# An attention and Hadamard-FFN kernel on one core: the first three output tiles formed group by group

## The chip, the cores and the metric

The kernel runs on one core of a Trainium2 chip. The metric is the device time of one execution in microseconds, as the median of several executions. A core has TensorE (PE: matmuls, and PEld: its weight loads), VectorE (DVE), ScalarE (ACT), GpSimd (POOL) and SyncE (SP), which in this kernel issues every DMA. Each engine works through its own instructions in order and waits on semaphores where it needs another's result.

## The reference

4096 rows of 512 go through linear attention with 16 heads of 128 in 4 key/value groups, an output projection `Wo`, an addition and a layer norm, then a gated FFN whose inputs are Hadamard transformed, an addition and a layer norm:

```python
qf = jax.nn.elu(q) + 1.0;  kf = jax.nn.elu(k) + 1.0      # after rotary embedding
def step(carry, inp):
    state, z = carry
    q_s, k_s, v_s = inp
    state = state + k_s[..., :, None] * v_s[..., None, :]
    z = z + k_s
    num = jnp.einsum('bhe,bhed->bhd', q_s, state)
    den = jnp.einsum('bhe,bhe->bh', q_s, z)[..., None] + EPS
    return ((state, z), num / den)
...
attn = out.transpose(1, 0, 2, 3).reshape(bsz, seq_len, H * HD) @ Wo.T
x = _layernorm(x + attn)
...
x = fwht(x * SU_ug) / SCALE
x = silu(x @ W_gate.T * s_gate) * (x @ W_up.T * s_up)
x = fwht(x * SU_dp) / SCALE
x = _layernorm(x_in + x @ W_down.T * s_down)
```

## The kernel before

All values are fp32. A matmul operand is split into a high half and a low remainder (`hilo`, L93: ACT copies the rounded high half, L94; DVE or POOL subtracts it from the value, L95), and each product is three matmuls: high by high, high by low, low by high.

**Attention** (L183 to L735) walks the sequence in blocks. Its 128 slots, `i` = 0 to 127, are a hand-written order: at each slot the source names what starts there, and instructions marked with `pin` or with a third argument `True` of `dma` keep their place in the order of the source. All other instructions are put in order by the compiler's scheduler, engine by engine. The attention leaves numerators (`num_d`, 32 tiles of 128 rows by 4 groups by 512) and denominators (`den_d`) in DRAM; denominators come back later, are inverted and stored as factors (`rec_d`).

**Output tiles** (L854 to about L1005). For each of 32 tiles of 128 rows and each of 4 groups of heads: numerators are loaded (`nt`), the factors are loaded and broadcast to 128 partitions (`rb`, `pre_rb`, L144), `norm_o` (L860) multiplies the two, on DVE for even groups into a PSUM tile `ps_on` and on POOL for odd ones into `o32`, and splits the product. `wo_tile` (L173) then runs 48 matmuls of 128 by 512 into one PSUM bank: 4 groups by 4 heads by 3. The tile is added to the rows of `x` in `yp`; every second tile a layer norm follows and a generator (`wo_front`) of Hadamard work for the FFN is started, which is stepped from tile to tile. Loads run ahead: `pre(t + 2)` opens tile `t + 2`'s numerators, one DMA of 1 MB, and `pre_rb` is eight groups ahead. A further generator, `constants` (L877), loads the sign and scale vectors and the Hadamard matrix (`sut`, `had32`, `wsc`, `sudp`, `wsdp`) and prepares them; it is stepped once per tile from tile 0 on.

**The seam between the two.** The output weights come as 16 raw tiles of 128 by 512, one for each head (`wo_raw`, L111), and are split by `wo_split` (L115). Both start before attention ends: raw loads at slots 118 to 123, splits of heads 0 to 10 at slots 121 to 126, of heads 11 to 15 behind the last slot (L722 to L726). Raw tiles borrow memory that attention has done with: `praw` buffers, the freed x halves (`xh`, `xl`), a `vd` tile for heads 10 to 13, and two quarters of `ntx` for heads 14 and 15. Tile 0's four groups are multiplied and split by `o_load`, `o_mul` and `o_split` (L505 to L527) between slots 107 and 126, and tile 0 is formed alone behind the last slot, in a PSUM bank of the attention's pool (`ps_w0`). Tile 1's numerators are read in four pieces of 256 KB (`nt_part`), tile 0's too; every other tile's as one DMA. The attention's PSUM pools close with attention, and the output tiles' pools (`pfd`, `pon`, `pwo`) are opened after that.

All DMAs stand on SP's queue in one order. A DMA that waits, for its source to be computed or for the last reader of the memory that it will write, holds back every DMA behind it. Pools opened with `reuse_waits="tile"` lay their tiles over memory of closed pools; the first write to such a tile waits for the last reader of whatever lay there.

Of the kernel before, what the change touches and what calls it, by code (L numbers as in the profile page):

```python
# [43 lines left out]
def kernel(  # L44
# [96 lines left out]

    RB = {}

    def pre_rb(k):  # L144
        if k < 128:
            pool, m = (late["p"], 3) if k < 6 or (k - 8) % 5 < 3 else (late["c2"], 2)
            RB[k] = pool.tile([128, 512], F32, tag="rb", name="rb", bufs=m)
            dma(RB[k], rec_d[k // 4][k % 4 * 512:k % 4 * 512 + 512].partition_broadcast(128), k < 10)

# [7 lines left out]
    def pre(t):  # L157
        if 5 <= t <= 13 and t % 2:
            if t > 5:
                recip(*cur["dn"])  # L160
            if t < 13:
                cur["dn"] = recip_load(NB - 4 + (t - 5) // 2)
        cur[t] = dict(nt=late["p"].tile([128, 16, 128], F32, tag="nt", name="nt", bufs=2))
        if t == 1:
            nt_part(0)
        else:
            dma(cur[t]["nt"], num_d[t].rearrange("p g n -> p (g n)"), t < 3)
        pre_yp(t)

    def nt_part(g):  # L170
        dma(cur[1]["nt"][:, 4 * g:4 * g + 4], num_d[1][:, g], True)

    def wo_tile(t, ps, after=None, gs=range(KVH)):  # L173
        i = 12 * gs[0]
        for g in gs:
            oh, ol = cur[t][g]
            for h in range(4):
                wh, wl = WO[4 * g + h]
                for l, r in ((oh, wh), (oh, wl), (ol, wh)):
                    T.matmul(ps, l[:, h], r, start=i == 0, stop=i == 47)  # L180
                    i += 1
            if after is not None:
                after(g)  # L183


    with ExitStack() as es:
# [4 lines left out]
        p3 = es.enter_context(tc.tile_pool(name="a3", bufs=3))  # L191
        pmm = es.enter_context(tc.tile_pool(name="pmm", bufs=3, space=PSUM))
        psc = es.enter_context(tc.tile_pool(name="psc", bufs=1, space=PSUM))
        pnum = es.enter_context(tc.tile_pool(name="pnum", bufs=2, space=PSUM))
        pden = es.enter_context(tc.tile_pool(name="pden", bufs=1, space=PSUM))
        pst = es.enter_context(tc.tile_pool(name="pst", bufs=1, space=PSUM))

# [307 lines left out]

        def o_load(g, hi, lo):
            if g < 2:
                nt = praw.tile([128, 512], F32, tag="raw", name="nt0")
                dma(nt, num_d[0][:, g], True)
                rb = praw.tile([128, 512], F32, tag="raw", name="rb0")  # L510
                dma(rb, rec_d[0][g * 512:(g + 1) * 512].partition_broadcast(128), True)
            else:
                nt = ntx[:, g]
                dma(nt, num_d[0][:, g], True)
                pre_rb(g)
                rb = RB.pop(g)
            O0[g] = (hi, lo, nt, rb)

        def o_mul(g, eng=G):
            pin(eng.tensor_tensor(O0[g][3], O0[g][2], O0[g][3], ALU.mult))  # L520

        def o_split(g, eng):
            hi, lo, nt, rb = O0[g]
            if hi is None:
                hi, lo = (wres.tile([128, 4, 128], F32R, tag="w", name=x) for x in ("oh0", "ol0"))
            hilo(hi, lo, rb.rearrange("p (h n) -> p h n", h=4), eng, True)
            cur.setdefault(g // 4, {})[g % 4] = (hi, lo)  # L527

# [62 lines left out]
        for i, (n, g, p) in enumerate(slots):  # L591
# [78 lines left out]
            elif i == 118:  # L670
                for h in range(3):
                    wo_raw(h, praw.tile([128, 512], F32, tag="raw", name="woraw"))
            elif i == 119:
                for x in ("xh", "xl"):
                    x = pe.tile([128, 4, 256], F32, tag=x, name="woraw").rearrange("p a b -> p (a b)")
                    wo_raw(len(WR), x[:, 0:512])
                    wo_raw(len(WR), x[:, 512:1024])
            elif i == 121:
                wo_split(G, 0, 1)
                wo_split(V, 2)  # L680
                for h in range(7, 10):
                    wo_raw(h, praw.tile([128, 512], F32, tag="raw", name="woraw"))
            elif i == 122:
                wo_split(G, 3, 4)
                wo_split(V, 5)
                o2 = [p3.tile([128, 2, 4, 128], F32R, tag=t, name=t, bufs=4) for t in ("qh", "ql")]
            elif i == 123:
                wo_split(G, 6)
                early.close()
# [3 lines left out]
                for y in range(2):  # L693
                    o_load(2 + y, o2[0][:, y], o2[1][:, y])
                x = p2.tile([128, 4, 512], F32, tag="vd", name="woraw")
                for h in range(10, 14):
                    wo_raw(h, x[:, h - 10])
                for h in range(14, 16):
                    wo_raw(h, ntx[:, h - 14])
                pre_rb(4)  # L700
                pre_yp(0)
                pre(1)
            elif i == 124:
                wo_split(G, 7)
                wo_split(V, 8)
            elif i == 125:
                o_mul(2, V)
                wo_split(G, 9)
                o_mul(3, V)
            elif i == 126:  # L710
                o_split(2, V)
                o_split(3, V)
                pre_rb(5)
                wo_split(G, 10)
            if sl == (1, 1):
# [5 lines left out]

        for g in range(1, KVH):  # L722
            nt_part(g)
        wo_split(V, 11)
        wo_split(G, 12)
        wo_split(V, 13)  # L726
        wo_split(G, 15)
        wo_split(V, 14)
        O0[4] = (*(p3.tile([128, 4, 128], F32R, tag=x, name=x) for x in ("sh", "sl")),
                 cur[1]["nt"][:, 0:4].rearrange("p h n -> p (h n)"), RB.pop(4))  # L730
        o_mul(4)
        o_split(4, V)
        ps0 = pmm.tile([128, DM], F32, tag="mm", name="ps_w0")
        wo_tile(0, ps0)
        pin(V.tensor_tensor(cur[0]["yp"][:, 0], ps0, cur[0]["yp"][:, 0], ALU.add))  # L735

# [116 lines left out]

    with ExitStack() as es:  # L854
        p2 = late["c2"] = es.enter_context(tc.tile_pool(name="c2", bufs=2, reuse_waits="tile"))
        pfd = es.enter_context(tc.tile_pool(name="pfd", bufs=1, space=PSUM, reuse_waits="tile"))
        pon = es.enter_context(tc.tile_pool(name="pon", bufs=2, space=PSUM, reuse_waits="tile"))
        pwo = es.enter_context(tc.tile_pool(name="pwo", bufs=3, space=PSUM, reuse_waits="tile"))

        def norm_o(t, g):  # L860
            c = cur[t]
            rb = RB.pop(4 * t + g).rearrange("p (h n) -> p h n", h=4)
            if g % 2 == 0:
                o32 = pon.tile([128, 4, 128], F32, tag="on", name="ps_on")
                i = V.tensor_tensor(o32, c["nt"][:, 4 * g:4 * g + 4], rb, ALU.mult)
            else:
                o32 = p2.tile([128, 4, 128], F32, tag="o32", name="o32")
                i = G.tensor_tensor(o32, c["nt"][:, 4 * g:4 * g + 4], rb, ALU.mult)  # L868
            hi, lo = (p2.tile([128, 4, 128], F32R, tag="o", name=n, bufs=8) for n in ("oh", "ol"))
            if t == 1:  # L870
                pin(i)
            hilo(hi, lo, o32, V, t == 1)
            c[g] = (hi, lo)

# [79 lines left out]
        raws = []  # L954
        for t in range(32):
            if t + 2 < 32:
                pre(t + 2)
            def after(g):
                if t == 31:
                    for s in (2 * g, 2 * g + 1):  # L960
                        if s < 7:
                            asplit(0, s)
                if t + 1 < 32:
                    if t + g:
                        norm_o(t + 1, g)
# [12 lines left out]
            if t < 3:  # L978
                next(gc, None)
            cur.pop(t)  # L980
            if t % 2:
# [409 lines left out]
```

## Time and profile before

| What | us |
|---|---|
| median of 3 runs | 2179.8 (2177.97, 2179.8, 2180.97) |
| the profiled execution | 2179.87 |
| its span in the profile | 2178.2 |
| mean granted TensorE clock in it | 0.997 of full |
| DRAM read, written | 282.76 MB, 156.76 MB |

The page divides the span into 40 slices; a slice is 54.5 us long. Its digits are tenths of busy time, so a 9 means 90% or more. Where the prediction shows a window, the columns are its bounds in microseconds from the span's start, its length, the busy time and number of instructions of each engine, the granted clock, the share of DMA time and the rate moved. In a timeline row the columns are the start, the busy time, the engine, the source line, the operation, what is written and read, and in brackets the idle time before it and who ended that. Attention ends at about 853 us; tile 1's matmuls begin at 864.37. These are, from the timelines of DVE, POOL and SP, products that use loaded factors, and the DMAs that carry factors and numerators (for a DMA, the time is that of its issue on SP's queue):

```profile
848.61 0.69 DVE L520 TENSOR_TENSOR rb<-ntx,rb 128x512 f32<-128x512 f32 x1 [1.13 <-DMA rb<-rec_d]
...
867.77 0.70 DVE L865 TENSOR_TENSOR ps_on<-nt,rb 128x512 f32<-128x512 f32 x1
...
873.77 0.70 DVE L865 TENSOR_TENSOR ps_on<-nt,rb 128x512 f32<-128x512 f32 x1 [0.92 <-DMA rb<-rec_d]
```

```profile
870.17 1.29 POOL L868 TENSOR_TENSOR o<-nt,rb 128x512 f32<-128x512 f32 x1 [5.27 <-DMA rb<-rec_d]
```

```profile
843.43 0.43 SPq L58 DMA_DIRECT2D rb<-rec_d  x1
...
864.22 0.80 SPq L58 DMA_DIRECT2D rb<-rec_d  x2
865.12 0.36 SPq L58 DMA_DIRECT2D nt<-num_d  x1
865.53 0.43 SPq L58 DMA_DIRECT2D yp<-in_x_n_dram  x1
866.00 1.67 SPq L58 DMA_DIRECT2D rb<-rec_d  x3
```

The factors issued at 843.43 are used at 848.61 on DVE, which waited for them (5.2 us); of the two issued at 864.22, the first is used at 867.77 by DVE, which was not waiting for anything else (at most 3.5 us), the second, issued at about 864.6, at 870.17 by POOL, which waited (5.6 us); the first of the three at 866.00, behind a 1 MB piece of numerators, at 873.77 by DVE, which waited (7.7 us).

### The profile page before, as it was taken

The page shows a single profiled execution, that of the slowest core. Times are in us where ns is not written, and L with a number is a line of the kernel's source. Part 1 is how long each engine was busy: PE and PEld are TensorE (multiplying, and loading weights), DVE is VectorE, ACT ScalarE, POOL GpSimd, SP SyncE. Part 2 cuts the span into 40 slices and gives each one's busy share as a digit, 9 for nine tenths or more (in the row PEclk, how much of TensorE's full clock was granted, in tenths as well). Part 3 has the DMA queues.
Part 4 walks back from the last instruction along what each step waited for, and adds up shares of the span by engine and source line. Part 5 has one row for each costly group of instructions (what it writes and reads, how often), then busy time and mean ns, then how long its engine had stood idle before and what let it go on. Part 6 is the DMA issues. An engine that isn't in the chain of part 4 may idle for free.

```text
span 2178.2 us, 42193 instructions
## 1 busy us (share of the span) xinstructions
PE 2140.6 (98%) x14319; PEld 1947.6 (89%) x14319; DVE 1728.9 (79%) x2675; ACT 1378.9 (63%) x2490; POOL 1321.8 (61%) x1104
## 2 busy tenths in 40 slices
PE   8999999999999998999999999999999999999998
PEld 8999999999999997887788788888888888999998
DVE  8999999899999997888998766776866766675655
ACT  8877877777777775443444476655655655565554
POOL 5777767666666666487888256565655555543332
PEclk9999999999999999999999999999999999999999
DMA  6666666656666666989988886876766767897784
GB/s 225 214 221 212 225 220 200 211 183 196 190 201 202 208 187 226 348 245 292 281 289 265 272 277 219 248 243 196 248 207 193 249 191 211 263 307 256 234 261 140
DMA packets 360553, 503.88 MB, mean 231 GB/s; under 512 B 68012, under 2 KB 187052, under 8 KB 356498
## 3 DMA queue, kind: packets, MB, share of 16 engines
q1 hardware_dynamic: 360338, 501.19, 72.1%
q8 instruction: 113, 1.85, 0.4%
q14 instruction: 102, 0.84, 0.1%
HBM read 282.76 MB, written 156.76 MB: 202 GB/s over the span
## 4 chain that ended last, share of the span: by engine, by line
PE 68%; DVE 12%; DMA 7%; issue 4%; POOL 4%; ACT 3%; SPq 2%; DVEq 0%; POOLq 0%; ACTq 0%
PE ps_a L1117 14%; PE ps_qk L339 12%; PE ps_da L1298 8%; PE ps_b L1117 7%; PE ps_wo L180 7%; PE ps_num L468 4%; PE ps_db L1298 4%; PE ps_c L1117 4%; PE ps_v L287 2%; DMA rb<-rec_d 2%; PE ps_dc L1298 2%; SPq L58 2%; DVE ps_qk L322 1%; PE ps_s L391 1%; DMA yraw<-yq_d 1%
## 5 line engine op out<-in xcount | busy, mean ns | idle before, releaser
L339 PE MATMUL ps_qk<-xh,wh 128*128 128x256 f32 x1280 | 354.9, 277 | 1.6 <-DVE x L325 0.9
L339 PE MATMUL ps_qk<-xh,wl 128*128 128x256 f32 x1280 | 354.0, 277 | 0.0
L339 PE MATMUL ps_qk<-xl,wh 128*128 128x256 f32 x1280 | 353.7, 276 | 0.0
L1099 POOL TENSOR_TENSOR cc<-cc 128x512 f32<-128x512 f32 x96 | 146.1, 1525 | 270.4 <-ACT cc L1096 129.5
L95 DVE TENSOR_TENSOR wol<-A,woh 128x512 fp32r<-128x512 f32 x217 | 226.4, 1050 | 94.7 <-ACT woh L94 84.0
L448 POOL TENSOR_SCALAR_AFFINE_SELECT A<-A 64x512 fp32r<-64x512 f32 x256 | 202.7, 792 | 131.1 <-DVE am L444 91.2
L321 POOL TENSOR_TENSOR sw<-sw,csb 128x512 f32<-128x512 f32 x160 | 213.9, 1337 | 76.2 <-ACT sw L320 64.8
L339 PEld LDWEIGHTS ps_qk<-xh,wh 128*128 128x128 f32 x1280 | 240.5, 188 | 4.7 <-DVE ql L422 1.5
L339 PEld LDWEIGHTS ps_qk<-xh,wl 128*128 128x128 f32 x1280 | 240.5, 188 | 1.5 <-DVE wl L95 0.2
L339 PEld LDWEIGHTS ps_qk<-xl,wh 128*128 128x128 f32 x1280 | 240.4, 188 | 1.0
L94 ACT ACTIVATE woh<-A 128x512 fp32r<-128x512 f32 x217 | 135.0, 628 | 122.5 <-PE ps_b L1117 72.8
L1117 PE MATMUL ps_a<-yoh,woh 128*128 128x512 f32 x512 | 199.9, 391 | 3.1 <-ACT sv L1124 2.6
L95 POOL TENSOR_TENSOR hal<-hraw,hah 128x512 fp32r<-128x512 f32 x74 | 98.1, 1327 | 172.7 <-PE ps_da L1298 59.6
L1117 PE MATMUL ps_a<-yol,woh 128*128 128x512 f32 x512 | 199.4, 389 | 0.0
L94 ACT ACTIVATE hah<-hraw 128x512 fp32r<-128x512 f32 x212 | 132.1, 631 | 106.3 <-PE ps_da L1298 54.2
L1117 PE MATMUL ps_a<-yoh,wol 128*128 128x512 f32 x512 | 196.7, 390 | 0.0
L95 DVE TENSOR_TENSOR hal<-hraw,hah 128x512 fp32r<-128x512 f32 x138 | 99.2, 727 | 90.1 <-PE ps_da L1298 39.0
L1124 ACT ACTIVATE sv<-ps_a,wsc 128x512 f32<-128x512 f32 x192 | 126.8, 679 | 34.7 <-PE ps_a L1117 34.4
L180 PE MATMUL ps_wo<-wh,oh 128*128 128x512 f32 x368 | 144.4, 393 | 0.0
L180 PE MATMUL ps_wo<-wh,ol 128*128 128x512 f32 x368 | 144.0, 391 | 0.0
L180 PE MATMUL ps_wo<-wl,oh 128*128 128x512 f32 x368 | 143.5, 390 | 0.0
L868 POOL TENSOR_TENSOR o<-nt,rb 128x512 f32<-128x512 f32 x62 | 86.8, 1400 | 74.0 <-DVE ol L95 44.1
(306 smaller groups left out, 7274.4 us busy)
## 6 DMA issues: line engine op xcount, KB each, us to landing
hraw<-hop_d SPq DMA_DIRECT2D x224, 256.0 KB
num_d<-num SPq DMA_DIRECT2D x128, 256.0 KB
rb<-rec_d SPq DMA_DIRECT2D x128, 256.0 KB
hop_d<-hS SPq DMA_DIRECT2D x128, 256.0 KB
vd<-vhl SPq DMA_DIRECT2D x128, 252.0 KB
nt<-num_d SPq DMA_DIRECT2D x30, 1024.0 KB
A<-in_wug_dram SPq DMA_DIRECT2D x93, 256.0 KB
hop_d<-cc SPq DMA_DIRECT2D x64, 256.0 KB
```

Of the source, the lines that this page charges most:

```text
L94: i = S.activation(hi, src, AF.Copy)
L95: j = eng.tensor_tensor(lo, src, hi.bitcast(F32), ALU.subtract)
L180: T.matmul(ps, l[:, h], r, start=i == 0, stop=i == 47)
L321: G.tensor_tensor(sw, sw, sinb, ALU.mult)
L339: T.matmul(ps[:, j], W[key][wa][:, k * 128:(k + 1) * 128], B[xa][:, k], start=i == 0, stop=i == 11)
L448: G.affine_select(ah, ah.bitcast(F32), pattern=[[0, 8], [1, 64]], compare_op=ALU.is_ge, fill=0.0, base=0, channel_multiplier=-1)
L468: T.matmul(ps[:, c2], l, r, start=i == 0, stop=i == len(ops) - 1)
L868: i = G.tensor_tensor(o32, c["nt"][:, 4 * g:4 * g + 4], rb, ALU.mult)
L1099: G.tensor_tensor(x, x, c.pop(("g", q)), ALU.mult)
L1117: T.matmul(ps, w[:, u, k], y[:, k], start=first and i == 0, stop=i == 5, skip_group_check=not first)
L1124: S.activation(x, ps, AF.Copy, scale=sc)
L1298: T.matmul(pj[j], ops[qd][al][:, r, js], BW[s][bl][ip], start=first and (i == 0 or i == 3 and pj is ps), stop=i >= 45 or last and i == 23, ...
```

## The change

The matmuls and what they compute stay the same. What is changed is the order of the first 12 of 128 pairs of tile and group, and with it where the output weights are split.

- `SQ` lists the pairs: for `k` = 0 to 11 tiles 0, 1, 2 of group 0, then tiles 0, 1, 2 of group 1, and so on; from `k` = 12 on tile by tile as before. `RB`, `NT` and `OH` (factors, numerators, split products) are kept by `k` and by pair.
- Tiles 0, 1 and 2 are summed in three PSUM banks at the same time (`PS`). For that the attention's PSUM pools close and the output tiles' pools open ahead of the first output matmul.
- `wo_part(0)` to `wo_part(4)` stand behind the last slot of attention, the others in a loop over `k`; `done` adds `x` at `k` = 9, 10 and 11, and goes on with what the loop over the tiles did.
- Output weights: heads 0 to 5 are split at slots 123 to 126, heads 6 and 7 behind the last slot, heads 8 to 15 between `wo_part` 0 and 5. Raw tiles 3 to 6 lie in `wres` buffers, 10 to 13 in the `vd` tile as before, 9, 14 and 15 in `praw`.
- Numerators of tiles 0, 1 and 2 are read in twelve pieces of 256 KB; from tile 3 on, as one DMA of 1 MB each.
- `constants` is stepped at `k` = 0, 4 and 8, behind `pre` of tiles 2, 3 and 4.

```diff
-    RB = {}
+    RB, NT, OH = {}, {}, {}
+    SQ = [(t, g) for g in range(KVH) for t in range(3)] + [(t, g) for t in range(3, 32) for g in range(KVH)]
+
+    def rb_src(k):
+        t, g = SQ[k]
+        return rec_d[t][g * 512:(g + 1) * 512].partition_broadcast(128)
+
+    def nt_src(k):
+        t, g = SQ[k]
+        return num_d[t][:, g]
 
     def pre_rb(k):
         if k < 128:
             pool, m = (late["p"], 3) if k < 6 or (k - 8) % 5 < 3 else (late["c2"], 2)
             RB[k] = pool.tile([128, 512], F32, tag="rb", name="rb", bufs=m)
-            dma(RB[k], rec_d[k // 4][k % 4 * 512:k % 4 * 512 + 512].partition_broadcast(128), k < 10)
+            dma(RB[k], rb_src(k), k < 10)
...
-        cur[t] = dict(nt=late["p"].tile([128, 16, 128], F32, tag="nt", name="nt", bufs=2))
+        nt = late["p"].tile([128, 4, 512], F32, tag="nt", name="nt", bufs=2)
+        for g in range(4):
+            NT[4 * t + g] = nt[:, g]
         if t == 1:
-            nt_part(0)
+            nt_part(4)
+        elif t == 2:
+            for k in range(8, 12):
+                nt_part(k)
         else:
-            dma(cur[t]["nt"], num_d[t].rearrange("p g n -> p (g n)"), t < 3)
+            dma(nt, num_d[t])
         pre_yp(t)
 
-    def nt_part(g):
-        dma(cur[1]["nt"][:, 4 * g:4 * g + 4], num_d[1][:, g], True)
+    def nt_part(k):
+        dma(NT[k], nt_src(k), True)
 
     def wo_tile(t, ps, after=None, gs=range(KVH)):
         i = 12 * gs[0]
         for g in gs:
-            oh, ol = cur[t][g]
+            oh, ol = OH.pop((t, g))
             for h in range(4):
                 wh, wl = WO[4 * g + h]
                 for l, r in ((oh, wh), (oh, wl), (ol, wh)):
                     T.matmul(ps, l[:, h], r, start=i == 0, stop=i == 47)
                     i += 1
             if after is not None:
-                after(g)
-
+                after(4 * t + g)
...
+        es_ps = ExitStack()
+        pmm = es_ps.enter_context(tc.tile_pool(name="pmm", bufs=3, space=PSUM))
+        psc = es_ps.enter_context(tc.tile_pool(name="psc", bufs=1, space=PSUM))
+        pnum = es_ps.enter_context(tc.tile_pool(name="pnum", bufs=2, space=PSUM))
+        pden = es_ps.enter_context(tc.tile_pool(name="pden", bufs=1, space=PSUM))
+        pst = es_ps.enter_context(tc.tile_pool(name="pst", bufs=1, space=PSUM))
...
+        def o_split(k, eng):
+            hi, lo, nt, rb = O0.pop(k)
             if hi is None:
                 hi, lo = (wres.tile([128, 4, 128], F32R, tag="w", name=x) for x in ("oh0", "ol0"))
             hilo(hi, lo, rb.rearrange("p (h n) -> p h n", h=4), eng, True)
-            cur.setdefault(g // 4, {})[g % 4] = (hi, lo)
+            OH[SQ[k]] = (hi, lo)
...
-            elif i == 119:
-                for x in ("xh", "xl"):
-                    x = pe.tile([128, 4, 256], F32, tag=x, name="woraw").rearrange("p a b -> p (a b)")
-                    wo_raw(len(WR), x[:, 0:512])
-                    wo_raw(len(WR), x[:, 512:1024])
             elif i == 121:
-                wo_split(G, 0, 1)
-                wo_split(V, 2)
-                for h in range(7, 10):
-                    wo_raw(h, praw.tile([128, 512], F32, tag="raw", name="woraw"))
+                for h in range(3, 7):
+                    wo_raw(h, wres.tile([128, 512], F32, tag="w", name="woraw"))
             elif i == 122:
-                wo_split(G, 3, 4)
-                wo_split(V, 5)
                 o2 = [p3.tile([128, 2, 4, 128], F32R, tag=t, name=t, bufs=4) for t in ("qh", "ql")]
             elif i == 123:
-                wo_split(G, 6)
+                wo_split(G, 0, 1)
                 early.close()
                 late["s"] = ExitStack()
                 late["p"] = late["s"].enter_context(tc.tile_pool(name="cl", bufs=2, side="right", reuse_waits="tile"))
                 ntx = late["p"].tile([128, 4, 512], F32, tag="nt", name="ntx", bufs=2)
                 for y in range(2):
                     o_load(2 + y, o2[0][:, y], o2[1][:, y])
+                for h in range(7, 9):
+                    wo_raw(h, praw.tile([128, 512], F32, tag="raw", name="woraw"))
+                pre_rb(4)
+                pre_yp(0)
+                pre(1)
                 x = p2.tile([128, 4, 512], F32, tag="vd", name="woraw")
                 for h in range(10, 14):
                     wo_raw(h, x[:, h - 10])
-                for h in range(14, 16):
-                    wo_raw(h, ntx[:, h - 14])
-                pre_rb(4)
-                pre_yp(0)
-                pre(1)
             elif i == 124:
-                wo_split(G, 7)
-                wo_split(V, 8)
+                wo_split(V, 2)
+                wo_split(G, 3)
+                wo_raw(9, praw.tile([128, 512], F32, tag="raw", name="woraw"))
             elif i == 125:
                 o_mul(2, V)
-                wo_split(G, 9)
+                wo_split(G, 4)
                 o_mul(3, V)
             elif i == 126:
                 o_split(2, V)
                 o_split(3, V)
                 pre_rb(5)
-                wo_split(G, 10)
+                wo_split(G, 5)
...
-        for g in range(1, KVH):
-            nt_part(g)
-        wo_split(V, 11)
-        wo_split(G, 12)
-        wo_split(V, 13)
-        wo_split(G, 15)
-        wo_split(V, 14)
-        O0[4] = (*(p3.tile([128, 4, 128], F32R, tag=x, name=x) for x in ("sh", "sl")),
-                 cur[1]["nt"][:, 0:4].rearrange("p h n -> p (h n)"), RB.pop(4))
+        es_ps.close()
+        wo_es = ExitStack()
+        pwo = wo_es.enter_context(tc.tile_pool(name="pwo", bufs=3, space=PSUM, reuse_waits="tile"))
+        pon = wo_es.enter_context(tc.tile_pool(name="pon", bufs=2, space=PSUM, reuse_waits="tile"))
+        pfd = wo_es.enter_context(tc.tile_pool(name="pfd", bufs=1, space=PSUM, reuse_waits="tile"))
+        PS = [pwo.tile([128, DM], F32, tag="wo", name="ps_w") for _ in range(3)]
+
+        def wo_part(k):
+            t, g = SQ[k]
+            wo_tile(t, PS[t], gs=[g])
+
+        O0[4] = (*(p3.tile([128, 4, 128], F32R, tag=x, name=x) for x in ("sh", "sl")), NT[4], RB.pop(4))
         o_mul(4)
         o_split(4, V)
-        ps0 = pmm.tile([128, DM], F32, tag="mm", name="ps_w0")
-        wo_tile(0, ps0)
-        pin(V.tensor_tensor(cur[0]["yp"][:, 0], ps0, cur[0]["yp"][:, 0], ALU.add))
+        wo_split(V, 6)
+        wo_split(G, 7)
+        for k in range(5, 8):
+            nt_part(k)
+        wo_raw(14, praw.tile([128, 512], F32, tag="raw", name="woraw"))
+        for k in range(5):
+            wo_part(k)
...
-    with ExitStack() as es:
+    with wo_es as es:
         p2 = late["c2"] = es.enter_context(tc.tile_pool(name="c2", bufs=2, reuse_waits="tile"))
-        pfd = es.enter_context(tc.tile_pool(name="pfd", bufs=1, space=PSUM, reuse_waits="tile"))
-        pon = es.enter_context(tc.tile_pool(name="pon", bufs=2, space=PSUM, reuse_waits="tile"))
-        pwo = es.enter_context(tc.tile_pool(name="pwo", bufs=3, space=PSUM, reuse_waits="tile"))
-
-        def norm_o(t, g):
-            c = cur[t]
-            rb = RB.pop(4 * t + g).rearrange("p (h n) -> p h n", h=4)
-            if g % 2 == 0:
+
+        def norm_o(k):
+            rb = RB.pop(k).rearrange("p (h n) -> p h n", h=4)
+            nt = NT.pop(k).rearrange("p (h n) -> p h n", h=4)
+            if k % 2 == 0:
                 o32 = pon.tile([128, 4, 128], F32, tag="on", name="ps_on")
-                i = V.tensor_tensor(o32, c["nt"][:, 4 * g:4 * g + 4], rb, ALU.mult)
+                i = V.tensor_tensor(o32, nt, rb, ALU.mult)
             else:
                 o32 = p2.tile([128, 4, 128], F32, tag="o32", name="o32")
-                i = G.tensor_tensor(o32, c["nt"][:, 4 * g:4 * g + 4], rb, ALU.mult)
+                i = G.tensor_tensor(o32, nt, rb, ALU.mult)
             hi, lo = (p2.tile([128, 4, 128], F32R, tag="o", name=n, bufs=8) for n in ("oh", "ol"))
-            if t == 1:
+            if k < 8:
                 pin(i)
-            hilo(hi, lo, o32, V, t == 1)
-            c[g] = (hi, lo)
+            hilo(hi, lo, o32, V, k < 8)
+            OH[SQ[k]] = (hi, lo)
...
-        for t in range(32):
-            if t + 2 < 32:
-                pre(t + 2)
-            def after(g):
-                if t == 31:
-                    for s in (2 * g, 2 * g + 1):
-                        if s < 7:
-                            asplit(0, s)
-                if t + 1 < 32:
-                    if t + g:
-                        norm_o(t + 1, g)
-                    pre_rb(4 * t + g + 8)
-
-            yp = cur[t]["yp"]
-            if t:
-                ps = pwo.tile([128, DM], F32, tag="wo", name="ps_wo")
-                wo_tile(t, ps, after)
-                V.tensor_tensor(yp[:, t % 2], ps, yp[:, t % 2], ALU.add)
-            else:
-                for g in range(KVH):
-                    after(g)
-            if t == 0:
-                gc = constants()
-            if t < 3:
-                next(gc, None)
-            cur.pop(t)
+
+        def after(k):
+            if k >= 124:
+                for s in (2 * (k - 124), 2 * (k - 124) + 1):
+                    if s < 7:
+                        asplit(0, s)
+            if 5 <= k + 4 < 128:
+                norm_o(k + 4)
+            pre_rb(k + 8)
+
+        def done(t, ps):
+            nonlocal fr, ylast
+            yp = cur.pop(t)["yp"]
+            V.tensor_tensor(yp[:, t % 2], ps, yp[:, t % 2], ALU.add)
...
+        ylast = None
+        gc = constants()
+        for k in range(12):
+            if k in (0, 4, 8):
+                pre(k // 4 + 2)
+                next(gc, None)
+            if k > 4:
+                wo_part(k)
+            after(k)
+            if k == 0:
+                wo_split(V, 8)
+                wo_raw(15, praw.tile([128, 512], F32, tag="raw", name="woraw"))
+            elif k == 1:
+                wo_split(G, 9)
+                wo_split(V, 10)
+            elif k == 2:
+                wo_split(G, 11)
+                wo_split(V, 12)
+            elif k == 3:
+                wo_split(G, 13)
+                wo_split(V, 14)
+            elif k == 4:
+                wo_split(G, 15)
+            if k > 8:
+                done(SQ[k][0], PS[SQ[k][0]])
+        for t in range(3, 32):
+            if t + 2 < 32:
+                pre(t + 2)
+            ps = pwo.tile([128, DM], F32, tag="wo", name="ps_wo")
+            wo_tile(t, ps, after)
+            done(t, ps)
```

More of the change, by code (lines that the diff above doesn't have):

```diff
@@ L191 @@
         p3 = es.enter_context(tc.tile_pool(name="a3", bufs=3))
[L192 to L196, printed above, removed]
+        es_ps = ExitStack()
[4 more added lines that the diff above has]
+        pst = es_ps.enter_context(tc.tile_pool(name="pst", bufs=1, space=PSUM))
         ones4 = p1.tile([128, 4], F32, name="ones4")
@@ L504, with o_load, o_mul @@
         O0 = {}
-        def o_load(g, hi, lo):
-            if g < 2:
+        def o_load(k, hi, lo):
+            if k < 2:
                 nt = praw.tile([128, 512], F32, tag="raw", name="nt0")
-                dma(nt, num_d[0][:, g], True)
+                dma(nt, nt_src(k), True)
                 rb = praw.tile([128, 512], F32, tag="raw", name="rb0")
-                dma(rb, rec_d[0][g * 512:(g + 1) * 512].partition_broadcast(128), True)
+                dma(rb, rb_src(k), True)
             else:
[L513 to L523, printed above, removed]
+                nt = ntx[:, k]
+                dma(nt, nt_src(k), True)
+                pre_rb(k)
+                rb = RB.pop(k)
+            O0[k] = (hi, lo, nt, rb)
+        def o_mul(k, eng=G):
+            pin(eng.tensor_tensor(O0[k][3], O0[k][2], O0[k][3], ALU.mult))
+        def o_split(k, eng):
+            hi, lo, nt, rb = O0.pop(k)
             if hi is None:
```

## The prediction

> **What bounds the kernel now.** I first read the page's busy shares, its slices and the chain that ended last.
>
> ```profile
> PE 2140.6 (98%) x14319; PEld 1947.6 (89%) x14319; DVE 1728.9 (79%) x2675; ACT 1378.9 (63%) x2490; POOL 1321.8 (61%) x1104
> ...
> PE   8999999999999998999999999999999999999998
> ...
> PE 68%; DVE 12%; DMA 7%; issue 4%; POOL 4%; ACT 3%; SPq 2%; DVEq 0%; POOLq 0%; ACTq 0%
> ```
>
> TensorE sets the time. A change that keeps its 14319 matmuls can only remove or add idle time and slow clock. The one inner slice under 9 is the sixteenth, 817 to 871 us: the seam between attention and output tiles, where the change lies. Next, windows cut at that seam:
>
> ```profile
> core 0: us, PE busy (x) PEld busy (x) DVE busy (x) ACT busy (x) POOL busy (x), PEclk, DMA share, GB/s
> 825.74:836.17 10.43, 5.88 (x51) 5.38 (x49) 9.14 (x13) 7.59 (x15) 8.00 (x9) 0.95 0.66 194
> 836.17:842.25 6.08, 6.05 (x27) 5.62 (x28) 5.92 (x10) 4.91 (x10) 5.32 (x5) 0.52 0.44 155
> 842.25:853.29 11.04, 10.86 (x68) 9.46 (x69) 7.46 (x11) 6.04 (x13) 10.03 (x11) 1.00 0.91 304
> 853.29:868.13 14.84, 11.56 (x44) 8.18 (x41) 7.96 (x11) 4.82 (x10) 7.51 (x5) 0.89 0.66 215
> 868.13:889.47 21.34, 21.34 (x97) 17.66 (x96) 13.79 (x28) 9.56 (x17) 6.44 (x5) 1.00 0.95 348
> ```
>
> Two windows lose PE time in idling and one (clock 0.52) in speed; from 868.13 PE is full. The timeline of PE, and of ACT and DVE, names the causes:
>
> ```profile
> 836.17 0.55 PE L434 MATMUL ps_sc<-qh,khl 128*128 128x256 f32 x1 [4.38 <-DVE A L445]
> ...
> 858.45 0.49 PE L180 MATMUL ps_w<-wh,qh 128*128 128x512 f32 x1 [2.47 <-ACT wh L94]
> 859.17 0.79 PE L180 MATMUL ps_w<-wl,qh 128*128 128x512 f32 x1 [0.23 <-DVE wl L95]
> ...
> 865.50 0.50 PE L180 MATMUL ps_wo<-wh,sl 128*128 128x512 f32 x1 [0.40 <-DVE sl L95]
> ```
>
> ```profile
> 857.03 0.60 ACT L472 ACTIVATE num<-ps_num 128x512 f32<-128x512 f32 x1 [3.63 <-DMA num_d<-num]
> ...
> 858.43 0.69 DVE L95 TENSOR_TENSOR wl<-woraw,wh 128x512 fp32r<-128x512 f32 x1 [4.51 <-ACT wh L94]
> ```
>
> The first idle (4.38) ends with the last attention block's chain on DVE, ahead of which POOL and DVE split output weights (DVE 1.41 at 830.68, POOL 2.54 at 829.00). The second (2.47) is tile 0, which needs all 16 heads' splits: ACT, in order, sat on the last numerators' buffer, and the splits stood behind it. After both, matmuls run at about half pace: 0.21 per 256 columns up to 842.25 (27 in 6.08; 3.1 at the usual 0.1135), some 0.42 per 512 columns from 858.45 to 863.1 (usual 0.2275). Last, SP's queue, on which every DMA is issued in order:
>
> ```profile
> 869.74 0.33 SPq L58 DMA_DIRECT2D sut<-in_su_ug_dram  x1
> 872.47 0.33 SPq L58 DMA_DIRECT2D had<-in_had_dram  x1
> 873.04 0.33 SPq L58 DMA_DIRECT2D wsc<-in_ws_ug_dram  x1
> 873.70 0.33 SPq L58 DMA_DIRECT2D sudp<-in_su_dp_dram  x1
> 874.39 0.33 SPq L58 DMA_DIRECT2D wsdp<-in_ws_dp_dram  x1
> 875.07 0.33 SPq L58 DMA_DIRECT2D nt<-num_d  x1
> ```
>
> Waits apart they follow each other at about 0.63 us ((875.07 − 872.47)/4 = 0.65).
>
> **The change, gains.** *Weight splits leave the end of attention.* Heads 0 to 5 are split there instead of 0 to 10, from slot 123 on, not 121. Gone from the first idle: DVE's split, 1.41, and the stretching of `ql` beside POOL (1.75 at 832.01 against 1.09 for the split at 864.35): 2.0. The idle left, 2.35, is like the 2.47 that also brought the slow clock, so only part of the slow clock goes: the first cost 6.05 − 3.1 = 3.0, the second 1.9 (11 matmuls in 4.65 less a gap of 0.23, at full pace 2.5); I take 0.5 of the 1.1 between. Sum 2.5 (bounds 0, if the chain waits for something else, and 2.0 + 3.0 = 5.0).
>
> *Tile 0's wait for all heads goes.* From 853.29 to 868.13 stand 41 matmuls by index. In the new order the same places hold k=0's rest to k=3 (tiles 0, 1, 2 of group 0, tile 0 of group 1; heads 0 to 7), split before: 41 × 0.2275 = 9.33 against 14.84, gain 5.5 (bounds 5.0 to 5.5, as nothing beats the pace). Lead at the end of k=3, called E: 8.0 (bounds 5.0 to 10.5).
>
> **The change, losses.** After E each k needs its own factors and, for k=3 onwards, weights of heads 4 to 15. In the changed kernel's instruction order the factor load of k=6 waits for k=3's last matmul: its buffer is opened over the memory of the q halves that k=3 reads. It lands E + 3.5 (the row at 864.22 is used at 867.77; other rows 5.2, 5.6, 7.7); product 0.70 and hi half 0.60 follow: k=6 starts at E + 4.85. PE holds 14 matmuls until then (k=4's rest, k=5): 14 × 0.2275 = 3.2. Stall 1.65. k=6 ends at E + 7.6.
>
> For k=7, in engine order: ACT's hi of head 11, POOL's low half of 11 (1.6) to E + 7.05, POOL's product 1.6 to 8.65, hi 0.6 to 9.25: stall 1.65, and 0.3 while its low half is late. k=7 ends at 12.25.
>
> For k=8 the constants come in between. The generator now starts at k=0; its four pinned loads (`had`, `wsc`, `sudp`, `wsdp`) stand on SP's queue ahead of k=8's factors. `had32` lies at the address of the raw tile of heads 10 to 13, so its load waits for DVE's split of 12 and POOL's of 13, which POOL reaches after k=7's product: 9.85 + 1.6 = E + 11.45. Behind it on SP stand wsc, sudp, wsdp, the factors of k=8, head 15's raw, the factors of 9 and 10. Four steps of 0.63 put k=8's factors out at E + 14; landing 4.5 (between 3.5 and 7.7, nearer the 5.2 and 3.5 of a queue with little in it), product and hi 1.3: k=8 starts at E + 19.8. PE ran dry at 12.25: stall 7.5 (bounds 5.4, with 3.5 for landing and quick issues, and 11). That is over 4.38, after which the trace lost 3.0 to the clock; after 2.47 some 1.9; I take 2.0 for this part and the two short stalls together (0 to 3.0).
>
> [...] The trace has the half rate after 2.47 already. [...]
>
> *Edits at nothing.* Three PSUM banks take the same 48 matmuls each; tile sums and layer norms of tiles 0 to 2 come later, under matmuls (DVE 13.79 of 21.34, ACT 9.56); uncovered, three additions and norms would be some 5 us. Twelve numerator pieces are three SP issues more (3 × 0.42), in SP's wait at `had`; uncovered 1.3. The constants' work on DVE stands ahead of k=8's product, but its loads land earlier.
>
> [...] Between 880 and 900 us the trace moves 400 GB/s, mostly in 256 KB loads. [...]
>
> **Sum.** −8.0 + 1.65 + 1.65 + 0.3 + 7.5 + 2.0 = +5.1. After tile 2 the prefetch is the old one, so nothing is won back. Profiled execution 2179.87 + 5.1 = 2185.0; the runs' median, 2179.8, is practically the same.
>
> **Rivals.** *A, faster: k=8 isn't held.* If `had` isn't late (heads 10 to 13 split early, or k=8's factors ahead of it), the last 7.5 and the clock go: −8.0 + 1.65 + 1.65 + 0.3 = −4.4, 2175.5. For it: one address decides. Against: the compiled order has the wait and the four loads ahead. It wins if k=8's factors are out before E + 6.4 (12.25 − 1.3 − 4.5).
> [...]
> *C, slower by more: landings.* k=6's factors at 5.6, k=8's at 7.7, as rows beside a 1 MB numerator have; tile 3's numerators do stand ahead of k=8's. +2.1 and +3.2 more: +10.4, 2190.3. It decides as soon as the queue carries more than 256 KB pieces there. Against: SP's own wait at `had` lets the queue drain.
> That the groups aren't formed in turn is excluded by the compiled order.
>
> **How the numbers follow.** Forecast 0.47 (its own range 2182.5 to 2187.5), A 0.10, B 0.25, C 0.18. The time is the forecast's, 2185.0. The range runs from 2179.0 (B's lower side; A outside) to 2190.5 (C). 0.2% is 4.4 us, about what measurement tells from no change: faster means under 2175.4 (A: 0.10); within, up to 2184.2 (B and 0.07 of the forecast: 0.32); slower the rest, 0.58.
>
> **What would show it.** In the new trace: a first idle near 2.35 before the last block's scores; no gap from attention to the fourth group; short gaps before the first `ps_w` of k=6 and k=7, released by DMA and POOL; one of about 7 before k=8, released by the chain POOL split, `had` load, factors, product; half-pace matmuls after it. Wrong if `had` goes out before POOL's split of head 13 matters, if the lead at E isn't 5 to 10, or if a gap appears behind tile 3.

## The result, and the profile after

| | before | changed |
|---|---|---|
| median, six runs of each | 2180.26 us | 2202.81 us |
| lowest, highest | 2177.97, 2183.58 | 2197.55, 2208.66 |
| ratio, 95% interval | | 1.0087 [1.0065, 1.0109] |
| profiled execution | 2179.87, span 2178.2 | 2200.59, span 2198.9 |

Slower, by 0.9%: on the forecast side, but four times the 5.1 us forecast (the profiled executions differ by 20.7 us) and far outside the range. Executions of these kernels, before's among them, fall into two groups some 10 us apart, whose difference shows in the last stage, behind 1.9 ms (443 matmuls from 2050 to 2100 us in the changed kernel's profile against 427 in e1's, the granted clock 1.00 in both), so kernels are compared below by ratios to the runs of before beside them, and by their profiles up to the FFN's first matmuls.

Both programs issue 14319 matmuls, so the start of the n-th matmul can be compared between them. This is worked out from the two traces (start after minus start before, us):

| n | 7000 | 7240 | 7260 | 7280 | 7400 | 8600 | 8700 | 8750 | 9000 | last |
|---|---|---|---|---|---|---|---|---|---|---|
| before, at | 818.9 | 867.2 | 871.8 | 876.3 | 902.7 | 1173.1 | 1195.0 | 1205.9 | 1264.6 | 2171.8 |
| changed | 1.1 | −7.3 | −3.0 | 5.2 | 10.2 | 9.1 | 11.3 | 19.5 | 20.2 | 20.9 |

A lead of 8.3 us is won (from 1.1 to −7.3), then 17.4 us are lost at the seam. From there to n = 8600 the lag hardly changes (10.2 to 9.1), and a second loss, 11.1 us, follows 300 us later, at 1173 to 1265 us, of which the prediction had nothing. Of the 20.9 us at the last matmul, 1.1 lie ahead of n = 7000, 9.1 are the seam's, 10.0 come between n = 7400 and 9000, 0.7 later.

The page's first lines, and windows of the changed kernel's profile, in the columns shown before:

```profile
PE 2146.7 (98%) x14319; PEld 1949.7 (89%) x14319; DVE 1729.7 (79%) x2675; ACT 1379.7 (63%) x2490; POOL 1318.6 (60%) x1104
...
PE   8999999999999997999999999999999999999998
```

```profile
core 0: us, PE busy (x) PEld busy (x) DVE busy (x) ACT busy (x) POOL busy (x), PEclk, DMA share, GB/s
...
853.00:860.83 7.83, 7.83 (x35) 6.08 (x33) 2.72 (x3) 2.94 (x6) 3.33 (x3) 1.00 0.77 252
860.83:880.86 20.03, 9.85 (x37) 6.29 (x37) 8.37 (x13) 5.63 (x11) 6.82 (x5) 0.95 0.88 284
880.86:888.20 7.34, 6.25 (x16) 4.57 (x16) 5.57 (x5) 2.92 (x5) 4.66 (x3) 0.66 0.46 149
...
1212.57:1217.69 5.12, 0.00 (x0) 0.00 (x0) 1.34 (x3) 0.18 (x1) 4.52 (x4) 0.93 1.00 322
1217.69:1223.80 6.11, 6.11 (x16) 4.90 (x17) 6.08 (x13) 1.10 (x5) 1.27 (x1) 0.50 1.05 267
```

The work of every engine is nearly the same; the slice of the seam, the sixteenth, fell from 8 to 7. PE is full from attention's end to 860.83, where before it stood idle: the wait for all sixteen heads is gone. Then PE is busy 9.85 of 20.03 us. At 1212.57 it stands still for 5.12 us and runs at clock 0.50 after it; in the kernel before PE is busy 59.09 of the 60 us from 1190 to 1250.

The seam, in PE's timeline of the changed kernel (brackets: idle before, and what ended it):

```profile
834.28 0.36 PE L448 MATMUL ps_sc<-qh,khl 128*128 128x256 f32 x1 [1.88 <-DVE A L459]
...
863.54 0.50 PE L194 MATMUL ps_w<-wh,oh 128*128 128x512 f32 x1 [2.71 <-ACT oh L94]
...
867.21 0.50 PE L194 MATMUL ps_w<-wh,oh 128*128 128x512 f32 x1 [0.39 <-ACT oh L94]
...
871.45 0.50 PE L194 MATMUL ps_w<-wh,oh 128*128 128x512 f32 x1 [0.96 <-ACT oh L94]
...
880.86 0.80 PE L194 MATMUL ps_w<-wh,oh 128*128 128x512 f32 x1 [6.12 <-ACT oh L94]
...
888.20 0.50 PE L194 MATMUL ps_w<-wx,ol 128*128 128x512 f32 x1 [1.09 <-DVE ol L95]
...
896.58 0.47 PE L194 MATMUL ps_wo<-wh,oh 128*128 128x512 f32 x1 [0.83 <-DVE yp L978]
```

These are the first matmuls of k = 5, 6, 7 and 8, the low half of k = 9, and tile 3. The long gap is followed back on SP's and POOL's timelines of the same profile:

```profile
867.53 0.33 SPq L58 DMA_DIRECT2D rb<-rec_d  x1
870.76 0.33 SPq L58 DMA_DIRECT2D nt<-num_d  x1
871.14 0.42 SPq L58 DMA_DIRECT2D rb<-rec_d  x1
871.61 0.42 SPq L58 DMA_DIRECT2D sut<-in_su_ug_dram  x1
873.31 0.33 SPq L58 DMA_DIRECT2D had<-in_had_dram  x1
873.69 0.43 SPq L58 DMA_DIRECT2D wsc<-in_ws_ug_dram  x1
874.17 0.43 SPq L58 DMA_DIRECT2D sudp<-in_su_dp_dram  x1
874.64 0.43 SPq L58 DMA_DIRECT2D wsdp<-in_ws_dp_dram  x1
875.12 0.43 SPq L58 DMA_DIRECT2D rb<-rec_d  x1
```

```profile
868.99 1.74 POOL L878 TENSOR_TENSOR o<-nt,rb 128x512 f32<-128x512 f32 x1
872.00 1.29 POOL L95 TENSOR_TENSOR wx<-woraw,wx 128x512 fp32r<-128x512 f32 x1 [1.26 <-ACT wx L94]
882.94 2.97 POOL L878 TENSOR_TENSOR o<-nt,rb 128x512 f32<-128x512 f32 x2 [9.65 <-DMA rb<-rec_d]
```

SP stands twice ahead of k = 8's factors, which go out at 875.12: first until 870.76, where tile 3's numerators wait until POOL's product of k = 7, the last reader of that buffer, ends (868.99 + 1.74 = 870.73), then until 873.31, where `had` waits for POOL's split of head 13 (872.00 + 1.29 = 873.29). Four issues of 0.4 us follow.

The second loss, from the timelines of PE, DVE, SP and POOL:

```profile
1217.69 0.80 PE L800 MATMUL ps_hd<-fhl,hadr 128*128 128x512 f32 x1 [5.12 <-DVE fhl L95]
```

```profile
1216.35 0.69 DVE L978 TENSOR_TENSOR yp<-ps_wo,yp 128x512 f32<-128x512 f32 x1 [10.67 <-DMA yp<-in_x_n_dram]
1216.96 0.68 DVE L95 TENSOR_TENSOR fhl<-ps_tr,fhl 128x512 fp32r<-128x512 f32 x1
```

```profile
1201.92 0.89 SPq L58 DMA_DIRECT2D rb<-rec_d  x2
1207.44 0.52 SPq L58 DMA_DIRECT2D wdop_d<-dbb  x1
1208.14 0.55 SPq L58 DMA_DIRECT2D yq_d<-ft  x1
...
1211.01 1.19 SPq L58 DMA_DIRECT2D yq_d<-ft  x2
1212.29 1.11 SPq L58 DMA_DIRECT2D yp<-in_x_n_dram  x2
```

```profile
1201.48 5.94 POOL L935 TENSOR_TENSOR dbb<-dbb 128x512 f32<-128x512 f32 x4
1207.38 0.73 POOL L822 TENSOR_TENSOR ft<-fq 128x256 f32<-128x256 f32 x1
```

From below: POOL ends four steps of the down weights' butterflies (sums and differences) at 1207.42; SP, which stood from 1202.81 at their store, issues it at 1207.44 and behind it stores of an FFN front, as POOL makes them; only then, at 1212.29, the rows of x (`yp`) of a tile pair. DVE, in order, waits 10.67 us for these, with the low half of the next front behind them, and PE waits for that.

### The profile page after: what moved, and what is told of

It is laid out like the page before. It is cut to its first block, busy times and chain, and to the rows that moved or that the text cites. A ratio compares the mean times of both kernels' runs of the same rounds, so it can differ in the third digit from the quotient of the medians.

```text
span 2198.9 us, 42202 instructions
## 1 busy us (share of the span) xinstructions
PE 2146.7 (98%) x14319; PEld 1949.7 (89%) x14319; DVE 1729.7 (79%) x2675; ACT 1379.7 (63%) x2490; POOL 1318.6 (60%) x1104
## 5 line engine op out<-in xcount | busy, mean ns | idle before, releaser
L194 PE MATMUL ps_wo<-wh,oh 128*128 128x512 f32 x348 | 136.7, 393 | 0.8 <-DVE yp L978 0.8
L194 PE MATMUL ps_wo<-wh,ol 128*128 128x512 f32 x348 | 136.1, 391 | 0.0
L194 PE MATMUL ps_wo<-wl,oh 128*128 128x512 f32 x348 | 136.1, 391 | 0.0
```

## The experiments

For each run the table gives, from its profile against that of before, the lag of its matmuls gained at the seam (from n = 7000 to 7400) and behind it up to the FFN's first matmuls (7400 to 9000), and how much of the latter falls behind n = 8600, where the changed kernel has its second loss. Then, from the compiled order (no time is in it), the number of the Hadamard matmul `ps_hd` that ends the first half of the last FFN front, and of the last matmul of the down-weight preparation, `ps_fd`. The ratios are to runs of the kernel before taken beside it.

| kernel | seam | behind it | of it from n = 8600 | last front | last preparation | ratio, 95% interval |
|---|---|---|---|---|---|---|
| before | 0 | 0 | 0 | 8714 | 8558 | 1 |
| changed | 9.1 | 10.0 | 11.1 | 8771 | 8613 | 1.0087 [1.0065, 1.0109] |
| e1 constants late | 0.5 | 11.1 | 10.9 | 8771 | 8613 | 1.0064 [1.0038, 1.0089] |
| e2 preparation early | 8.4 | 20.4 | 13.6 | 8776 | 8558 | 1.0114 [1.0080, 1.0147] |
| e3 both | 0.0 | 19.5 | 11.8 | 8776 | 8558 | 1.0088 [1.0060, 1.0116] |
| e4 before, preparation late | −0.1 | 0.2 | 4.6 | 8742 | 8617 | 0.9976 [0.9950, 1.0002] |
| f1 changed, 3 steps | 10.5 | 3.6 | 8.9 | 8626 | 8758 | 1.0063 [1.0040, 1.0086] |
| f2 e1 and 3 steps | 0.2 | 4.6 | 9.2 | 8626 | 8758 | 1.0016 [0.9994, 1.0038] |
| f3 before, 3 steps | 0.5 | 3.5 | 4.9 | 8584 | 8709 | 0.9999 [0.9975, 1.0023] |
| f4 f2, two waits less | 1.0 | 5.5 | 9.8 | 8626 | 8758 | 1.0026 [1.0003, 1.0048] |
| h1 e1, 3 and 4 steps in turn | −0.4 | −4.4 | 1.5 | 8663 | 8619 | 0.9977 [0.9956, 0.9998] |
| h2 early preparation, 3 steps | 1.3 | −0.3 | 2.7 | 8636 | 8566 | 0.9985 [0.9961, 1.0010] |
| h3 h1 and k = 5's numerators early | −0.2 | −4.4 | 1.5 | 8663 | 8619 | 0.9977 [0.9955, 0.9999] |
| h4 before, 3 and 4 steps in turn | 0.1 | −6.3 | −0.4 | 8639 | 8596 | 0.9957 [0.9932, 0.9982] |

**First round: is the second loss an echo of the first, or late side work?**

e1, the constants behind k = 8's factors:

```diff
             if k in (0, 4, 8):
                 pre(k // 4 + 2)
+            if k in (5, 8, 9):
                 next(gc, None)
```

> The changed kernel with the generator of the constants stepped at k = 5, 8 and 9 instead of 0, 4 and 8, so that the factors of k = 8 stand on SP's queue ahead of the constants and of tile 3's numerators. Theory T (two losses: at the seam the wait of k = 8 for its factors; near 1210 us the side work of the output tiles, which began some 20 us late on POOL and whose stores hold SP's queue ahead of the x rows): the gap of 6.1 before k = 8 and the half pace after it (2.6) go, some 8 us, the stall near 1210 stays, 2192 (2189 to 2196). Rival R1 (the stall near 1210 is only the seam's delay showing again): both go, 2181 to 2186. Rival of the seam (the gap is the latency of a full queue, not the order): gap stays above 4, 2198 or more.

The seam fell from 9.1 to 0.5: SP's order was the cause of the long gap, which is gone from the trace (1.72 before k = 6, 0.96 and 1.02 at k = 7, none at k = 8). In the compiled order tile 3's numerators moved behind k = 8's factors too, so this run doesn't part the two waits. The second loss stayed whole, with the same row:

```profile
1210.84 0.79 PE L800 MATMUL ps_hd<-fhl,hadr 128*128 128x512 f32 x1 [5.36 <-DVE fhl L95]
```

R1, the echo, has fallen. In the profiles the lag won between n = 7000 and 9000 fell from 19.1 to 11.6, by 7.5 us, near T's 8; the ratio fell by 0.0023, some 5 us, but its interval overlaps the changed kernel's.

e2 begins the preparation earlier, e3 adds e1's edit, e4 delays it in the kernel before:

```diff
-            if t == 2:
-                draw_next()
-                draw_next()
-            if t >= 3:
+            if t >= 2:
                 step(gd, 4)
...
+            if k == 7:
+                draw_next()
+                draw_next()
```

> The changed kernel with the first two loads of down-projection weights issued at k = 7 instead of behind tile 2, and that preparation stepped from tile 2 on instead of 3; the constants as changed. T: the seam is as in the changed kernel (about 10 us behind before at tile 3), the loss near 1210 is gone or below 3: 2190 (2188 to 2194). R1: the loss near 1210 stays, since the seam's delay is there: 2199 or more. R2 (the loss near 1210 comes of another order of the instructions at the tail, not of late side work): 2197 or more.

> Both edits together. T: seam near even (between 1 us ahead of before and 4 behind at tile 3), no loss near 1210: 2181 (2178 to 2185). R1: the same as with the constants alone. R2: the loss near 1210 stays, 2190.

In e4 the conditions are `t == 3` and `t >= 4`.

> The kernel before, nothing of the groups, with the same side work a tile later: first two loads of down-projection weights behind tile 3 instead of 2, stepping from tile 4 instead of 3 (about 11 us). T: the seam is untouched, a stall appears between 1190 and 1270 us: 2186 (2183 to 2190). R1 and R2: no change, 2178 to 2182.

Theory T missed the times of all three. In e2 and e3 the preparation ends where it does in before (8558), and the loss near 1210 us is there all the same (13.6 and 11.8), with 6.7 and 7.7 us more lost ahead of n = 8600; so a late preparation isn't its cause. R2, another order at the tail, fits them best. In e4 the last preparation stands at 8617, later than the changed kernel's 8613; the kernel comes out level (0.2), but by 4.5 us won ahead of n = 8600 and 4.6 lost behind it, with a gap of 1.88 us at 1205.04. That gap is not a held queue: DVE, on which PE waited for a front's low half, worked through a layer norm's small operations from 1199.43 to 1204.31. What the kernels that lose 10 us or more share is the last front at 8771 or 8776, a tile's worth behind before's 8714.

**Second round: the fronts.** One edit, fewer steps of the preparation for each tile, lets the compiler's scheduler put the fronts sooner:

```diff
             if t >= 3:
-                step(gd, 4)
+                step(gd, 3)
```

> The changed kernel with the preparation of the down weights stepped 3 times a tile instead of 4, nothing else: in the compiled order the last two FFN fronts (their Hadamard matmuls) move from the 8687th and 8771st matmul to the 8523rd and 8626th (before: 8630th and 8714th), the last of the preparation from the 8613th to the 8758th. Theory F (the loss near 1210 us comes of the fronts: after the group order they stand a tile later against the output matmuls, because POOL and DVE began the side work late and are nearly full; the x rows of a late pair wait for the front that read their buffer, behind its stores on SP): the seam's loss of 9 stays, the loss between 1190 and 1270 us falls from 9 to under 2: about 9 below the changed kernel's profiled 2201, near 2192. Rival P (the loss comes of the preparation being late): it grows, 2201 or more. Rival R1 (the seam's delay showing again): no change.

> The same with the constants stepped at k = 5, 8 and 9. F: both losses gone, at the end within 4 us of before: 2180 to 2184. P: 2192 or more.

> The kernel before with the preparation stepped 3 times a tile, as a control. F: before has little to lose near 1210 us (PE is full there), so no change, or up to 3 us less from the small gaps between 1010 and 1090 us: 2177 to 2181. P: slower by 3 or more.

f4 is f2 with:

```diff
-            pool, m = (late["p"], 3) if k < 6 or (k - 8) % 5 < 3 else (late["c2"], 2)
+            pool, m = (late["p"], 3) if k < 7 or (k - 8) % 5 < 3 else (late["c2"], 2)
...
                 pre_rb(5)
+                nt_part(5)
```

and `pre_rb(6)` behind the last slot.

> The second of these with two more waits taken from the seam: the numerators of k = 5 are loaded where the factors of k = 5 are, ahead of the last numerator stores, and the factors of k = 6 go into the ring of the factors of k = 2 to 5 instead of the memory of the q halves, loaded behind the last slot. F: the gaps before k = 5 (1.2 to 2.7) and k = 6 (0.4) go, those before k = 7 stay: 1.5 to 4 us below the second kernel, 2176 to 2181, a little faster than before or level.

The stall near 1210 us went, as F had it, but another came some 30 us later: f2 is 4.1 us ahead of before at n = 8700 and 6.7 behind at 8900. F's loss of under 2 wasn't met (8.9 and 9.2 from n = 8600); f1 and f2 are better than the changed kernel and e1 mostly by what they win ahead of that. f2's ACT, POOL and SP timelines say why:

```profile
1236.50 1.06 ACT L94 ACTIVATE yoh<-yraw 128x1024 fp32r<-128x1024 f32 x1 [10.60 <-DMA yraw<-yq_d]
```

```profile
1221.73 5.72 POOL L935 TENSOR_TENSOR dbb<-dbb 128x512 f32<-128x512 f32 x3
```

```profile
1227.48 0.57 SPq L58 DMA_DIRECT2D wdop_d<-dbb  x1
1229.17 0.33 SPq L58 DMA_DIRECT2D araw<-was_d0S  x1
1229.55 0.55 SPq L58 DMA_DIRECT2D araw<-in_wug_dram  x1
1230.19 0.55 SPq L58 DMA_DIRECT2D yraw<-yq_d  x1
```

Now the preparation ends last (8758), and its store, which goes out at 1227.48 when POOL is done at 1227.45, holds the loads of the FFN's first inputs (`yraw`); ACT waits 10.60 us for them, with the high half of a product for the output tiles behind them, and PE 4.66. It is the same mechanism with other loads behind the held store. Before with 3 steps (f3) is level by its ratio, as F had it, while its profile is 3.5 us behind, as P had it, with a gap of 3.23 us near 1226; there DVE, on whose low half PE waits, is busy 17.90 of the 18 us from 1211 to 1229: a full engine, not a held queue. f4's gaps before k = 5 and k = 6 went, but low halves late on DVE took their place (2.33 and 2.99 us at k = 7 and 8): no gain, where 1.5 to 4 us were expected.

**Third round: neither may end last.** 3 and 4 steps in turn, `step(gd, 3 + t % 2)`, put fronts at 8663 and preparation at 8619.

> The changed kernel with the constants at k = 5, 8 and 9 and the preparation of the down weights stepped 3 and 4 times a tile in turn. In the compiled order the last front and the last of the preparation stand at the 8663rd and 8619th matmul; with 4 steps they stand at 8771 and 8613, with 3 at 8626 and 8758, in the kernel before at 8714 and 8558. Theory B (refined after the runs with 3 steps, where the stall moved from 1206 to 1235 us and the loads behind SP's held queue were those of the FFN's first inputs instead of the x rows: whichever side work ends last, its stores from POOL hold SP's queue and the loads behind them; so the loss is gone when both, fronts and preparation, end as early as in before): no stall over 2 us between 1190 and 1270 us, level with or ahead of before at the FFN's first matmul (between 3 us ahead and 2 behind): 2176 to 2182. Rival (POOL's delay is conserved, so a stall comes back whatever the order): 4 us or more behind, 2184 or more.

> The changed kernel with the constants at k = 5, 6 and 7, the first loads of down weights at k = 6, the preparation stepped 3 times at k = 8 to 11 and 3 times a tile from tile 3. Last front and last preparation stand at 8636 and 8566. B: no stall near 1210 to 1240; at the seam the added loads and splits may cost up to 3: 2176 to 2184. Rival: as the kernel with 3 and 4 steps in turn.

h2 has instead 3 steps a tile, the constants at k = 5, 6, 7, first loads of down weights at k = 6 and 3 steps at each of k = 8 to 11; h3 is h1 with `nt_part(5)` early.

> The first of these with the numerators of k = 5 loaded ahead of the last numerator stores. The gap before k = 5 (1.1 to 2.7 in the runs so far) goes: up to 2 us below the first, 2175 to 2181; no difference if the next wait, that of k = 7, takes it up.

> Control: the kernel before with 3 and 4 steps in turn. B: before has no held queue to free, so within 3 us of before: 2177 to 2182.

h1 is ahead of before, 0.9977; the second loss is gone with the groups left as they are (1.5 us from n = 8600, against e1's 10.9). Its window has PE busy 58.69 of 60 us where the held queue had been:

```profile
1190.00:1250.00 60.00, 58.69 (x257) 47.62 (x255) 43.61 (x74) 28.25 (x46) 20.82 (x17) 1.00 0.81 265
```

h2 has no gap over 1 us from 1190 to 1270 either and is level with before, as B had it. h3 is no faster than h1, since the next wait takes its place (1.76 us before k = 6). The control gained more than was expected, 0.9957: among others, before's gaps of 2.05 us near 1011 and 1.16 near 1086 went. It parts two effects of the pacing. Between n = 7400 and 8600 both kernels win some 6 us by it (h4 5.9; h1 5.9, where e1 has 0.2 lost), which has nothing to do with the groups; behind n = 8600 it takes 9.4 us from the loss of e1, and 0.4 from before. The lowest ratio of all kernels here is thus that of the one before with the preparation at 3 and 4 steps; between it and h1 the intervals overlap, so the groups neither win nor cost anything that these runs can tell, once the constants are out of the way and the preparation is paced.

## Why the prediction was wrong, point by point

- *Lead at E, 8.0*: measured 8.3, of it 3.0 by n = 7200, the end of attention (2.5 forecast), and 5.3 behind it (5.5). The first idle fell from 4.38 to 1.88 (2.35 forecast), and half pace still followed it, as forecast (clock 0.50 from 835 to 838 us); the wait for all heads went.
- *Losses at the seam, 13.1*: measured 17.4. By start-to-start times less one matmul of 0.2275: k = 5 2.87 (forecast: none), k = 6 0.55 (1.65), k = 7 1.12 (1.95 with its low half), k = 8 6.28 (7.5), half pace after it 2.43 (2.0), low half of k = 9 1.27 and tile 3 0.99 (both: none). These make 15.5; most of the remaining 1.9 lies in waits under 0.3 us. The mechanism of k = 8 was right, and e1 confirms it; its factors went out at 875.12, 15 us behind the end of k = 3 near 860 (14 forecast). The forecast had nothing of SP's wait at tile 3's numerators for POOL's k = 7; as the wait at `had` ends later (873.31 against 870.76), it added nothing here. k = 5's gap is a piece of numerators issued at 856.31, behind the last numerator stores, and used by POOL at 861.56: the pieces, priced at nothing, weren't free at that place; what their size costs no run here shows.
- *"After tile 2 the prefetch is the old one, so nothing is won back"* and *"tile sums and layer norms of tiles 0 to 2 come later, under matmuls"*: this is the step that failed, and the prediction's own sign of being wrong, a gap behind tile 3, came. It took the two kernels to run level behind tile 3, at no cost, where 10.0 us were lost; it priced these additions and norms, but not what they start. The first front's products on POOL moved from 905.8 to 926.1 us, the first loads of down weights from 887.7 to 906.5. Of these 20 us, about half are the seam's; the rest is the group order, which ends the first pair of tiles with the third tile (in e1, level at the seam, the two are at 917.7 and 899.3, still some 12 us late). The compiled order then has the last front 57 matmuls later, and a queue held by a front's stores and the preparation's cost 10 us. e1 shows that this loss stays when the seam's is gone; h1, with h4 as its control, that it goes when the side work alone is paced otherwise. That the late start is what shifts the last front by a whole tile, over 1500 matmuls, is argued (from 950 to 1000 us DVE is busy 42.63 and POOL 43.36 of 50), not shown: no run moves the fronts' start alone, and that the scheduler simply found another order (R2) fits as well.
- *Rivals.* A's lever was real, though not by `had` alone: e1 frees the seam, but to level, not to 4.4 ahead, since k = 5, 6 and 7 give the lead back. B put the end near even by a lead of 10 and no half pace behind the stall of k = 8, a term that no run shows: the lead was 8.3, the clock 0.52 followed the 6.12 us, and a near-even seam came only with the long stall gone (0.5 in e1). C named longer landings; k = 8's factors landed in 4.4 us (875.12 to the product at 879.48; 4.5 forecast). None had a place beyond tile 3.
- *The slow clock.* In the changed kernel the gap of 6.12 us ahead of k = 8 brought half pace, as forecast (clock 0.52 for 5.16 us, to 886.02), and so did the 5.12 us from 1212.57 (clock 0.50 for 6.11 us, to 1223.80). The shorter gaps of 2.71, 0.39 and 0.96 us, ahead of 863.54, 867.21 and 871.45, didn't (clock 1.00 in the 12 matmuls behind each), but before's gap of 2.47 us did (clock 0.63 from 858.45 to 863.10).

## What to carry to other kernels

When a reordering makes a stage's first results later, price what they start, not only themselves: here the loss came out 300 us later, at the other end of the stage. On a queue that issues all transfers in order, look for stores of a late producer ahead of loads that the critical engines need; pacing the producer can move the wait to the next loads instead of removing it, so look at what ends last. And before crediting a reordering, give the old order the same pacing: here that alone gave the lowest ratio.

## What wasn't expected of the hardware

In these profiles the length of a gap alone doesn't tell whether half pace follows. It did behind 1.88 us (changed kernel, clock 0.50 from 835.00 to 838.00 us) and 2.47 us (kernel before, clock 0.63 from 858.45 to 863.10), not behind 2.71 us (changed kernel, clock 1.00 from 863.54 to 866.50), and did behind 5.12 and 6.12 us. At the same place in attention it didn't behind 2.48 us in the kernel before (clock 1.00 from 436.71 to 440.71) and did behind 2.47 us in the changed one (clock 0.59 from 438.02 to 442.02).
